# Image 2's norm, the gate's copies and residual's taps, and the order of the attention's sums in a fused mamba, attention and expert kernel

## The chip, the cores and the metric

The kernel runs on one core of a Trainium2 chip. The metric is the device time of one execution in microseconds (us), taken as the median of the runs shown. Each core has TensorE (PE, with weight loads listed apart as PEld), VectorE (DVE), ScalarE (ACT), GpSimd (POOL) and SyncE (SP, which issues most of the transfers here). [...]

## The reference

The input is four images of 256 channels by 1024 positions in float32. Cut to what matters here (LN is a norm over channels):

```python
xs = LN(x)                                     # over the 256 channels, then again with norm_w, norm_b
xc = split(xs into 4 groups of 64 channels)
xm = mamba(xc) + skip * xc                     # selective scan over the 1024 positions
Q  = conv1x1(depthwise3_grouped(xm))           # qdw, qpw
xg = sigmoid(Q) * xm                           # gates
R  = conv1x1(depthwise3(xg)) + xg              # rdw, rpw ("residual")
cat = [xs, R]
xm2 = conv1x1(depthwise3(cat)) + xs            # fdw, fpw ("mixing")
x_out = gelu(LN([depthwise3(xm2), mha(xm2)] @ fc + fc_b))
x  = x + proj(LN(dwconv3x3(LN_hw(x_out))))
t  = tokens(x); x = t + top2_experts(LN(t))    # 8 experts, 256 -> 1024 -> 256
```

`mha` has 8 heads of 32 channels. The mamba scan has, for each group, 128 inner channels by 16 states: `h = exp(dt * A) * h + dt * u * B`, and the output is the sum of `h * C` over the states.

## The kernel before, in words

Channels lie on the 128 partitions in two chunks c (0 and 1), positions along the free axis in two halves h of 512.

**The scan.** For each image b (0 to 3), group n (0 to 3) and half h there is a part of 16 steps i: 32 parts in one long row. A step is four operations on four engines: the decay dA on ACT (L718, an exp of dts), the inflow dBu on DVE (L728, written into a PSUM slot), the scan hs on DVE (L739), and the product of hs with C on POOL (L747). PE adds the products up (L757), spreads B over the partitions (L710), and projects u for the next part (L616, L622). SP loads dts and the C rows ahead (L681, L704). At a part's end ACT copies y out (L764) and POOL multiplies it by z (L765). Each part also prepares the next one: the Silu of u and z (L642, L646, with a table load before and after), and dt (L661 to L668).

**What runs beside it.** Other stages are written as generators. A part's loop advances every running generator after its instructions, and `yield k` means "I have nothing for k ticks". The order of each engine's queue is thus fixed by where the `yield`s stand. `in_turn(items, make, use, lag, every)` issues `make` for an item and `use` for the item `lag` ticks back. The stages of image b run beside image b+1: `convolutions(b)` starts with the first part of image b+1 and mostly falls into the parts (b+1, 0, 0) and (b+1, 0, 1); `attention(b)` starts after a few parts, when the preparation of q, k and v is done. The scan stops while the attention runs and resumes when `attended` is set, three steps before the attention's end. Image 3 has no scan beside it (`beside` is false). Behind it come the expert tiles, from 1676 us to the end.

**Slots.** PSUM tiles come from one ring of 8 banks for everything (`ps`), halves in SBUF from rings of 16 (`a2`) and full rows from 4 (`a4`). A tile that takes a slot waits for the last reader of the tile that had it before.

**Norm.** `normalised(b)`: means by matmul with `ones_mean` (`column_mean`, L438), subtraction on DVE (L536), squares on POOL (L546), variances by L438 again, the root on ACT, then for each chunk a POOL product xl (L556), a DVE product xn (L558), a POOL scale (L561), and for images 2 and 3 `own_taps` (L572 on ACT and twice L579 on DVE; image 3's are taken later from a stored copy). A float32 matmul shows as two records in the trace. The norm of image 1 runs beside the scan, that of image 2 beside attention 0, that of image 3 beside attention 1.

**Gate, residual and mixing.** `convolutions(b)` makes qd on PE (L921), copies it on ACT (qs, L928), multiplies by qpw on PE (gp, L935), copies it on ACT (g, L944), takes the sigmoid (L949), and multiplies xm by the gates on POOL (L957). `depthwise3` then forms residual's three taps: one on ACT (L457) and two on DVE (L462) for each chunk. The projections follow (`rp`, `fx`, `fp`, L426 and L428), with copies on ACT: own L976, residual L994, mixed L968. `prepared` computes v and then q and k, copied on ACT by L1101.

**Attention.** A step is a pair of a group and a half with one of eight key tiles kt: four logit matmuls (L1126), four exps on ACT (L1136), four value matmuls (L1175). DVE adds the exps of an even and an odd step (L1183), and `sum_pair` (L1147) sums the pair on PE with a matmul of ones.

Of the kernel before, what the change touches and what calls it, by code (L numbers as in the profile page):

```python
# [10 lines left out]
AF = mybir.ActivationFunctionType  # L11
ALU = mybir.AluOpType
# [4 lines left out]
NC2 = C // P  # L17
HH = WW = 32
N = HH * WW
# [59 lines left out]
def network(  # L79
# [27 lines left out]
    nc = tc.nc  # L107
    shifted = sums is None
    B = x.shape[0]
# [16 lines left out]
    def col(name, i=0, rows=slice(0, P)):  # L126
        at = _AT[name] + i
        return V[rows, at : at + 1]
# [22 lines left out]
    with tc.tile_pool(name="w_conv", bufs=1) as wp, tc.tile_pool(  # L151
# [248 lines left out]
        def a4(name, shape=(P, N)):  # L400
            return act4.tile(list(shape), F32, tag="a4", name=name)

        def a2(name, rows=P):
            return act2.tile([rows, HALF], F32, tag="a2", name=name)

        def half(h):
            return ts(h, HALF)
# [26 lines left out]
        def column_mean(name, chunks):  # L434

            out = ps(name)
            for ci, chunk in enumerate(chunks):
                nc.tensor.matmul(  # L438
                    out, ones_mean, chunk, start=(ci == 0), stop=(ci == len(chunks) - 1)
                )  # L440
            return out

        def in_turn(items, make, use, lag=2, every=1):

            made, lag = [], lag // every
            for at in range(len(items) + lag):
                if at >= lag:
                    use(items[at - lag], made[at - lag])
                if at < len(items):
                    made.append(make(items[at]))  # L450
                yield every
# [71 lines left out]
        def normalised(b):  # L523


            place_xn(b)
            xn = XN[b]

            def part(c, h):
                return xn[:, c, ds(LEFT + h * HALF, HALF)]  # L530

            yield 4

            def centre(h, mean):
                for c in range(NC2):
                    nc.vector.tensor_tensor(part(c, h), part(c, h), mean, ALU.subtract)  # L536

            yield from in_turn(
                range(2), lambda h: column_mean(f"mean_{b}_{h}", [part(c, h) for c in range(NC2)]),
                centre,  # L540
            )
            r1, r2 = a4(f"r1_{b}"), a4(f"r2_{b}")
            for h in range(2):
                sq = [a2(f"sq_{b}_{h}_{c}") for c in range(NC2)]
                for c in range(NC2):
                    nc.gpsimd.tensor_tensor(sq[c], part(c, h), part(c, h), ALU.mult)  # L546
                yield 1
                var = column_mean(f"var_{b}_{h}", sq)
                yield 2
                root(r1[:, half(h)], var, eps6)  # L550
                yield 1
                root(r2[:, half(h)], var, eps11, scale=1.0 + 1e-5)
                yield 1
            for c in range(NC2):
                xl = a4(f"xl_{b}_{c}")
                nc.gpsimd.tensor_tensor(xl, xn[:, c, LEFT:], r1, ALU.mult)  # L556
                yield 2
                nc.vector.tensor_tensor(xn[:, c, LEFT:], xn[:, c, LEFT:], r2, ALU.mult)  # L558
                yield 1
                nc.sync.dma_start(XL[b][:, c, :], xl)  # L560
                nc.gpsimd.tensor_scalar(  # L561
                    xn[:, c, LEFT:], xn[:, c, LEFT:], col("norm_w", c), col("norm_b", c),
                    ALU.mult, ALU.add,
                )
                yield 1
                if b in XD and b < B - 1:
                    yield from own_taps(b, c, xl)
# [330 lines left out]
        def convolutions(b):  # L898
# [19 lines left out]
            for k in range(3):  # L918
# [5 lines left out]
                        start=(k == 0), stop=(k == 2),  # L924
                    )
                yield 1 if k else 0
            yield 1
            nc.scalar.activation(qs, qd, AF.Identity, bias=qdw_b)  # L928
            yield 1
            def gate(c):  # L930
# [23 lines left out]
            def gating():  # L954
                yield from in_turn(range(NC2), gate, keep)
                for c in range(NC2):
                    nc.gpsimd.tensor_tensor(  # L957
                        xm[:, c, 1 : N + 1], gs[c], xm[:, c, 1 : N + 1], ALU.mult
                    )
                    yield 1  # L960
                for c in range(NC2):
                    yield from depthwise3(d[1], c, xm, c, "rdw_w", c, col("rdw_b", c))

            def mixed(at, r):
                co, h = at
# [48 lines left out]
            for c in range(NC2):  # L1014
                for ticks in depthwise3(
# [11 lines left out]
                    ],  # L1027
                    xl[:, at[0], ds(1 + at[1] * HALF, HALF)] if beside else None,
                    NC2 if beside else 0,
                ), mixed, lag=2 if b == B - 1 else 4, every=1 if b == B - 1 else 2,  # L1030
            )
            yield from prepared(b)

# [73 lines left out]
        def attention(b):  # L1107

            v8, qk = QKV.pop(b)
            rows = [
                largest(b, g, qk[g][:, 0, :], qk[g][:, 1, :]) if shifted else None
                for g in range(2)
            ]
            yield 1
            steps = [(g, h, kt) for g in range(2) for h in range(2) for kt in range(NK)]

            def logits(g, h, kt):  # L1120

                q, k = qk[g][:, 0, :], qk[g][:, 1, :]
                sts = [ps(f"st_{b}_{g}_{h}_{kt}_{i}") for i in range(4)]
                for i in range(4):
                    r = ts(i, HD)
                    nc.tensor.matmul(  # L1126
                        sts[i], k[r, ts(kt, P)], q[r, half(h)], start=True, stop=not shifted
                    )
                    if shifted:
                        nc.tensor.matmul(  # L1130
                            sts[i], ones[HD * i : HD * i + 1, :],
                            rows[g][HD * i : HD * i + 1, half(h)], start=False, stop=True,
                        )
                es = [a2(f"e_{b}_{g}_{h}_{kt}_{i}") for i in range(4)]
                for i in range(4):
                    ins = nc.scalar.activation(es[i], sts[i], AF.Exp, scale=1.0 / HD**0.5)  # L1136
                T["exps"] = ins if b == B - 1 else None
                return es

            log_exp()  # L1140
            ahead = logits(*steps[0])
            pairs, accs, ending = [], [None, None], []

            def sum_pair():
                kt, acc, es = pairs.pop()
                for i in range(4):
                    nc.tensor.matmul(  # L1147
                        acc[ts(i, HD)], ones[:, 0:HD], es[i], start=(kt == 1), stop=(kt == NK - 1)
                    )

            def end_block(g, h, values, total):

                low, out = a2(f"low_{b}_{g}_{h}"), OT[b][g][:, half(h)]
                at = (2 * b + g) * 2 + h
                nc.scalar.activation(low, total, AF.Ln, bias=added)
                if shifted:
                    nc.scalar.activation(low, low, AF.Exp, scale=-1.0)
                else:
                    nc.vector.tensor_reduce(sums[:, 0, at : at + 1], total, AX.X, ALU.max)
                    nc.scalar.activation(  # L1160
                        low, low, AF.Exp, scale=-1.0, accum_out=sums[:, 1, at : at + 1]
                    )
                nc.vector.tensor_tensor(out, values, low, ALU.mult)

            for at, (g, h, kt) in enumerate(steps):
                es = ahead
                if pairs and (kt % 2 or at > len(steps) - 6):
                    sum_pair()
                if at + 1 < len(steps):
                    ahead = logits(*steps[at + 1])  # L1170
                if kt == 0:

                    accs = [ps(f"av_{b}_{g}_{h}_{w}") for w in range(2)]
                for i in range(4):
                    nc.tensor.matmul(  # L1175
                        accs[0][ts(i, HD)], v8[:, kt, ts(4 * g + i, HD)], es[i],
                        start=(kt == 0), stop=(kt == NK - 1),
                    )
                if kt % 2 == 0:
                    first = es  # L1180
                else:
                    for i in range(4):
                        nc.vector.tensor_tensor(first[i], first[i], es[i], ALU.add)  # L1183
                    pairs.append((kt, accs[1], first))
                    if ending:
                        end_block(*ending.pop())
                if kt == NK - 1:
                    ending.append((g, h, *accs))
                if at == len(steps) - 3:
                    T["attended", b] = True  # L1190
                yield 1
            sum_pair()
            yield 1
            end_block(*ending.pop())
            yield 1
# [1324 lines left out]
```

## Time and profile before

| what | value |
|---|---|
| median of 3 runs | 2168.41 us (2166.26 to 2169.15) |
| profiled execution | 2167.03 us, span 2165.3 us |
| granted TensorE clock | 0.961 of full speed |
| attention 0, 1, 2, 3 (from the windows of the trace, about) | 99, 101, 94, 83 us |
| tail of the experts (1676 to 2165 us) | PE busy 458.64 of 489 us |
| L747 POOL product | 512 times, 1339 ns mean |
| L718 ACT decay | 512 times, 718 ns mean |

The page lists each engine's busy time over the whole span, then the span in 40 slices, the costliest groups of instructions, and what ended the idle time before them. A window of the trace gives the same busy times for a stretch. A timeline line gives the start, the duration, the engine, the line of the kernel and its operation, and in brackets the idle time of the engine just before, with what ended it.

### The profile page before, as it was taken

What the parts mean: (1) busy time and instruction counts of PE and PEld (TensorE: products, weight loads), DVE (VectorE), ACT (ScalarE), POOL (GpSimd) and SP (SyncE); (2) the same over time, 40 slices, a digit from 0 to 9 for tenths busy, and PEclk for the clock granted to TensorE, in tenths of its full rate; (3) what the DMA queues carried; (4) which work ended last, traced back from release to release, by engine and by line L of the source; (5) the groups of instructions that cost most, each with busy time, mean ns of one, the idle gap of its engine ahead of it and who ended that gap; (6) DMA issues with size and microseconds to landing.
All of it is one profiled execution on the core that took longest, in us unless ns stands there. A gap on an engine that the chain in (4) does not pass through costs nothing. (4 is left out here: it accounts for less than half of the span.)

```text
span 2165.3 us, 28187 instructions
## 1 busy us (share of the span) xinstructions
PE 1931.0 (89%) x8690; PEld 867.6 (40%) x8690; DVE 1540.5 (71%) x2252; ACT 1212.3 (56%) x2272; POOL 1043.4 (48%) x931
## 2 busy tenths in 40 slices
PE   6778778999977999988779999669999989999996
PEld 2113112322211332223123223216652668888885
DVE  4989999957998989698899888987265354321121
ACT  4665657668777677776466876615268423222221
POOL 0887887812787850476877016662021012522131
PEclk8888999999999999998999999989999999999998
DMA  3555544401444431153634203444230165777764
GB/s 105 148 157 130 124 118 103 101 28 57 103 116 117 104 75 40 25 141 92 176 87 105 83 6 94 109 164 135 84 99 23 47 198 161 242 229 188 213 184 131
DMA packets 157087, 251.40 MB, mean 116 GB/s; under 512 B 34740, under 2 KB 101332, under 8 KB 156664
## 3 DMA queue, kind: packets, MB, share of 16 engines
q1 hardware_dynamic: 136560, 223.47, 37.3%
q0 software_dynamic: 12720, 17.32, 4.1%
q10 hardware_dynamic: 7640, 8.65, 1.2%
q8 instruction: 72, 1.18, 0.2%
q14 instruction: 95, 0.78, 0.1%
HBM read 137.22 MB, written 36.62 MB: 80 GB/s over the span
## 5 line engine op out<-in xcount | busy, mean ns | idle before, releaser
L747 POOL TENSOR_TENSOR dA<-hs,cs 128x512 f32<-128x512 f32 x512 | 681.1, 1339 | 376.9 <-DVE hs L739 249.8
L718 ACT ACTIVATE dA<-dts,A 128x512 f32<-128x512 f32 x512 | 359.0, 718 | 161.4 <-DMA dts<-dt 76.9
L757 PE MATMUL yp<-dA,quads 128*32 128x512 f32 x1024 | 286.3, 640 | 89.3 <-POOL dA L747 76.6
L2350 POOL DMA_INDIRECT Y<-ys,dest x68 | 109.6, 1612 | 424.3 <-DVE ys L2343 417.3
L1136 ACT ACTIVATE e<-st 128x512 f32<-128x512 f32 x512 | 263.7, 606 | 89.4 <-PE st L1126 89.2
L2337 ACT ACTIVATE hs<-h,b 128x256 f32<-128x256 f32 (+1 forms) x256 | 110.6, 478 | 343.6 <-PE h L2332 256.7
L728 DVE TENSOR_TENSOR dBu<-dts,bs 128x512 f32<-128x512 f32 x384 | 259.6, 677 | 46.0 <-PE bs L710 10.8
L739 DVE TENSOR_TENSOR_SCAN hs<-dA,last,dBu 128x512 f32<-128x512 f32 x192 | 243.6, 1269 | 3.0 <-issue 2.1
L2365 PE MATMUL y<-w,hs 128*128 128x256 f32 (+1 forms) x1088 | 242.4, 382 | 0.0
L2332 PE MATMUL h<-xT,w 128*128 128x256 f32 (+1 forms) x1024 | 239.7, 390 | 0.8 <-DVE xT L2295 0.8
L739 DVE TENSOR_TENSOR_SCAN hs<-dA,dBu 128x512 f32<-128x512 f32 x192 | 231.6, 1206 | 0.7 <-PE var L438 0.7
L1183 DVE TENSOR_TENSOR e<-e,e 128x512 f32<-128x512 f32 x256 | 168.2, 718 | 77.8 <-ACT e L1136 47.8
L2332 PEld LDWEIGHTS h<-xT,w 128*128 128x128 f32 x1024 | 195.2, 192 | 41.7 <-issue 8.0
L2365 PEld LDWEIGHTS y<-w,hs 128*128 128x128 f32 (+1 forms) x1088 | 197.3, 188 | 36.1 <-issue 9.0
L2295 DVE COPY xT<-xp 128x512 f32<-128x512 f32 (+1 forms) x36 | 23.3, 646 | 249.4 <-PE xp L2291 249.1
L710 PE MATMUL bs<-u,xpwT_s 128*32 128x512 f32 x1024 | 162.9, 669 | 40.3 <-DVE hs L739 17.3
L1126 PE MATMUL st<-qk 32*128 32x512 f32 x1024 | 174.0, 638 | 0.3
L757 PEld LDWEIGHTS yp<-dA,quads 128*32 128x32 f32 x1024 | 51.3, 114 | 303.4 <-POOL dA L747 198.7
L1175 PE MATMUL av<-e,v 128*32 128x512 f32 x1024 | 139.5, 604 | 0.0
L1953 POOL DMA_INDIRECT XS<-XR,to x64 | 65.4, 1022 | 92.0 <-ACT e L1136 53.9
L1126 PEld LDWEIGHTS st<-qk 32*128 32x128 f32 x1024 | 59.5, 183 | 115.3 <-issue 85.6
L1147 PE MATMUL av<-e,every 128*32 128x512 f32 x512 | 85.2, 596 | 2.7 <-DVE e L1183 2.6
(357 smaller groups left out, 2640.5 us busy)
## 6 DMA issues: line engine op xcount, KB each, us to landing
dts<-dt SPq DMA_DIRECT2D x512, 128.0 KB
w<-in_W_dram SPq DMA_DIRECT2D x124, 512.0 KB
cs<-cd SPq DMA_DIRECT2D x512, 64.0 KB
xs<-XS SPq DMA_DIRECT2D x32, 260.0 KB
xd<-xn SPq DMA_DIRECT2D x64, 128.0 KB
xn<-in_x_dram SPq DMA_DIRECT2D x8, 512.0 KB
XL<-xl SPq DMA_DIRECT2D x8, 512.0 KB
xl<-XL SPq DMA_DIRECT2D x4, 1024.0 KB
```

The costliest lines, as they stand in the source:

```text
L710: nc.tensor.matmul(bs[r], xpwT_s[:, n, s : s + 1].to_broadcast([P, 32]), T[b, n, "u"][:, half(h)], start=True, stop=True,)
L718: nc.scalar.activation(dA, T[b, n, h, "dts", g][:, 0, :], AF.Exp, scale=A[:, g, n, q : q + 1])
L728: nc.vector.tensor_tensor(dBu, T[b, n, h, "dts", g][:, 1, :], T[b, n, h, "bs", q], ALU.mult)
L739: nc.vector.tensor_tensor_scan(hs, T[b, n, h, "dA", i], dBu, 0.0 if h == 0 else last, ALU.mult, ALU.add)
L747: nc.gpsimd.tensor_tensor(dA, hs, T[b, n, h, "cs", q], ALU.mult)
L757: nc.tensor.matmul(T[b, n, h, "yp"][ts(g, 32)], quads, T[b, n, h, "dA", q * GD + g], start=False, stop=(q == GS - 1),)
L1126: nc.tensor.matmul(sts[i], k[r, ts(kt, P)], q[r, half(h)], start=True, stop=not shifted)
L1136: ins = nc.scalar.activation(es[i], sts[i], AF.Exp, scale=1.0 / HD**0.5)
L1175: nc.tensor.matmul(accs[0][ts(i, HD)], v8[:, kt, ts(4 * g + i, HD)], es[i], start=(kt == 0), stop=(kt == NK - 1),)
L1183: nc.vector.tensor_tensor(first[i], first[i], es[i], ALU.add)
L2332: nc.tensor.matmul(hp[:, i, :], w1(c, k0 + i), xT[:, c, :], start=(c == 0), stop=(c == NC2 - 1))
L2365: nc.tensor.matmul(yp[ts(k % parts, n), ts(t % 2, C)], hidden(k)[:, ds(t * P, n)], w2(k), start=(k < parts), stop=(k >= NHC - parts),)
```

## The change

There are four edits.

1. In the norm of image 2 alone, POOL adds the two chunks of each half before the mean and adds the two squares before the variance, so that `column_mean` has one chunk to multiply. The sums use the tiles r1 and r2 in place of four half tiles. The generator takes four more ticks.
2. The qs copy comes one tick later for images 0 to 2. Residual's taps are written out: first tap of chunk 0 on ACT, an idle tick, first tap of chunk 1 on ACT, then four taps on DVE, a tick each.
3. The mixing copies have a lag of 2 in place of 4 for images 0 to 2 (still every second tick).
4. The sum of a pair is issued after the value matmuls of the next step; only for image 2 (`late`) is it issued at the head of the step after that, as it was for all images before.

```diff
@@ normalised(b)
+            r1, r2 = a4(f"r1_{b}"), a4(f"r2_{b}")
+            one_chunk = b == 2
+            if one_chunk:
+                for h in range(2):
+                    nc.gpsimd.tensor_tensor(r1[:, half(h)], part(0, h), part(1, h), ALU.add)
+                yield 2
             yield from in_turn(
-                range(2), lambda h: column_mean(f"mean_{b}_{h}", [part(c, h) for c in range(NC2)]),
+                range(2), lambda h: column_mean(
+                    f"mean_{b}_{h}",
+                    [r1[:, half(h)]] if one_chunk else [part(c, h) for c in range(NC2)],
+                ),
                 centre,
             )
-            r1, r2 = a4(f"r1_{b}"), a4(f"r2_{b}")
             for h in range(2):
-                sq = [a2(f"sq_{b}_{h}_{c}") for c in range(NC2)]
+                if one_chunk:
+                    sq = [v[:, half(h)] for v in (r1, r2)]
+                else:
+                    sq = [a2(f"sq_{b}_{h}_{c}") for c in range(NC2)]
                 for c in range(NC2):
                     nc.gpsimd.tensor_tensor(sq[c], part(c, h), part(c, h), ALU.mult)
+                if one_chunk:
+                    nc.gpsimd.tensor_tensor(sq[0], sq[0], sq.pop(), ALU.add)
+                    yield 1
                 yield 1
                 var = column_mean(f"var_{b}_{h}", sq)
@@ convolutions(b)
-            yield 1
+            yield 2 if beside else 1
             nc.scalar.activation(qs, qd, AF.Identity, bias=qdw_b)
...
+                def first_tap(c):
+                    nc.scalar.activation(
+                        d[1][:, c, :], xm[:, c, 0:N], AF.Identity, bias=col("rdw_b", c),
+                        scale=col("rdw_w", 3 * c),
+                    )
+
+                first_tap(0)
+                yield 1
+                yield 1
+                first_tap(1)
                 for c in range(NC2):
-                    yield from depthwise3(d[1], c, xm, c, "rdw_w", c, col("rdw_b", c))
+                    for k in (1, 2):
+                        nc.vector.scalar_tensor_tensor(
+                            d[1][:, c, :], xm[:, c, k : k + N], col("rdw_w", 3 * c + k),
+                            d[1][:, c, :], ALU.mult, ALU.add,
+                        )
+                        yield 1
...
-                ), mixed, lag=2 if b == B - 1 else 4, every=1 if b == B - 1 else 2,
+                ), mixed, lag=2, every=1 if b == B - 1 else 2,
@@ attention(b)
+            late = b == B - 2
...
-                if pairs and (kt % 2 or at > len(steps) - 6):
+                if late and pairs and (kt % 2 or at > len(steps) - 6):
                     sum_pair()
                 if at + 1 < len(steps):
                     ahead = logits(*steps[at + 1])
...
+                if pairs and not late:
+                    sum_pair()
                 if kt % 2 == 0:
                     first = es
```

## The prediction

> **What bounds the kernel now.** I read the page's busy shares, then a table by stage, then the idle gaps of whichever engine is full in each stage. The chain that ended last is no help: it holds only the final stores. The shares are averages over unlike stages:
>
> ```profile
> PE 1931.0 (89%) x8690; PEld 867.6 (40%) x8690; DVE 1540.5 (71%) x2252; ACT 1212.3 (56%) x2272; POOL 1043.4 (48%) x931
> ```
>
> The table by stage (columns: window, length, busy us and count of PE, PEld, DVE, ACT, POOL, then clock and DMA) for the convolution part of image 0, the scan behind it, attention 0, and the convolution part of image 2:
>
> ```profile
> 332.00:374.00 42.00, 38.71 (x136) 12.30 (x136) 37.08 (x39) 28.49 (x44) 33.90 (x22) 0.96 0.35 85
> 374.00:435.00 61.00, 57.52 (x226) 22.50 (x226) 58.32 (x65) 43.32 (x81) 49.77 (x41) 1.00 0.44 108
> 435.00:534.00 99.00, 98.60 (x650) 27.77 (x650) 64.02 (x84) 75.89 (x147) 15.27 (x11) 1.00 0.09 32
> 1084.00:1128.00 44.00, 37.86 (x131) 11.87 (x134) 39.95 (x38) 27.69 (x43) 34.34 (x29) 0.96 0.34 83
> ```
>
> Read it so: in an attention PE is full (98.60 of 99.00) and POOL nearly idle; in the scan DVE is full (58.32 of 61.00). The convolution parts are the scan with holes in DVE. The holes (timeline of DVE; the bracket is the idle time before and who ended it), for images 0 and 2; image 1 at 690.90 and 704.13 repeats image 0 within 0.1 us:
>
> ```profile
> 332.09 0.69 DVE L728 TENSOR_TENSOR dBu<-dts,bs 128x512 f32<-128x512 f32 x1 [0.22 <-ACT g L944]
> 346.19 1.88 DVE L462 SCALAR_TENSOR_TENSOR d<-xm,V,d 128x1024 f32<-128x1024 f32 x1 [4.02 <-ACT d L457]
> 1083.70 0.70 DVE L728 TENSOR_TENSOR dBu<-dts,bs 128x512 f32<-128x512 f32 x1 [5.42 <-ACT g L944]
> 1096.83 5.43 DVE L462 SCALAR_TENSOR_TENSOR d<-xm,V,d 128x1024 f32<-128x1024 f32 x1 [4.02 <-ACT d L457]
> 1103.97 2.79 DVE L462 SCALAR_TENSOR_TENSOR d<-xm,V,d 128x1024 f32<-128x1024 f32 x1
> ```
>
> So residual's first tap stops the scan for 4.0 us in each of three images, and in image 2 an inflow stops for 5.4 us more. ACT shows why the inflow waits: its own queue stands.
>
> ```profile
> 1075.35 0.69 ACT L928 ACTIVATE qs<-qd,qdw_b 128x512 f32<-128x512 f32 x1 [4.99 <-PE qd L921]
> 331.38 1.25 ACT L944 ACTIVATE g<-gp,V 128x512 f32<-128x512 f32 x2
> 333.49 0.72 ACT L718 ACTIVATE dA<-dts,A 128x512 f32<-128x512 f32 x1 [0.86 <-DMA dts<-dt]
> ```
>
> In attention 0 the var matmuls sit in a full PE, and one block of sums is torn apart (its eight matmuls start at 523.62 and the next logits at 526.65: 3.03 us, where the undisturbed block at 520.69 is followed after 0.97):
>
> ```profile
> 466.35 1.98 PE L438 MATMUL var<-sq,ones_mean 128*128 128x512 f32 x4
> 523.62 1.66 PE L1147 MATMUL av<-e,every 128*32 128x512 f32 x6
> 525.68 1.05 PE L1147 MATMUL av<-e,every 128*32 128x512 f32 x2 [0.40 <-DVE e L1183]
> 526.65 1.14 PE L1126 MATMUL st<-qk 32*128 32x512 f32 x8
> ```
>
> [...] Here the 592 ns var matmuls follow each other every 0.48 us (466.35 to 468.26 for four), so I price them at the pitch. [...] this trace has 1.28. The change adds no load.
>
> **The change, part by part** (in us, minus is faster).
>
> *Norm of image 2, in attention 0.* A mean and a variance per half take one matmul instead of two: four matmuls go, each two records, so eight records of the sixteen. Eight records at 0.48 are 3.8, on a full PE: −3.8. POOL gets four adds of 128x512; its L747 product of that size takes 1.27, so 5.1 in a stage where it is busy 15.27 of 99: hidden. The added ticks push the tail later. In the changed order the second chunk's L558 product and both its L579 taps come after the first steps of the next scan part, where before only the last tap did: two more DVE operations (about 1.2 and 1.28) in a stage where DVE is the bound: +2.4. In return DVE is free at the end of the attention, and the torn block at 523.62 should close: −2.0 (bounds −2.3 and 0). SP's store of XL_2 now stands in its queue among the cs and dts loads of that part and waits for POOL; if a load is held, dA waits: 0 to +3, taken as 0, because loads are issued some steps ahead.
>
> *Sums.* Outside image 2 the sum of a pair is issued at the end of the even step, not at the head of the odd one. Inside an attention that is the same PE order; what changes is that other streams' matmuls (op, mean, var) come behind the sum instead of before it, and that the last inner pairs of the last block are summed one logits-and-values later. At 466.35 var covered 1.98 us in which DVE was adding e (L1183); without that cover the sum can stand at the head of PE: between 0 and 2 per such place, four places in attention 0, most with the adds done long before: +1.5. The late pairs only gain time, counted in the −2.0 above. Attention 1's and 3's stalled sums wait for DVE, which the edit leaves as it is: 0.
>
> *qs copy and g copies.* The qs copy L928 goes behind the table load and Silu, and the first decays. In image 2 it then no longer holds ACT for 4.99. But all gate work comes a step later: on ACT the order becomes dA_2, dA_3, g, g, dA_4, where it was dA_2, g, g, dA_3. The inflow of step 1 takes the PSUM slot of the first gp in both kernels, so it waits for the first g copy. At image 0, dA_3 cannot start before 333.49 (its DMA); 333.49 + 0.72 + one g copy of 0.68 gives 334.9 instead of 332.09: +2.8, and the same for image 1. At image 2 Silu is bound by its up matmuls (L622 ends at 1074.26) once the qs copy no longer stands ahead of it: 1074.3 + 1.15 + 1.08 + 1.29 (Silu, its second line, the load, by the starts 1077.35 to 1080.87) = 1077.8, then dA_0, qs, dA_1, dA_2 and dA_3 at 0.71 each, then one g copy: 1082.0, where the inflow started at 1083.70: −1.7.
>
> *Taps.* In the new order the four DVE taps follow hs6, hs7, hs8, hs9 (before hs4, hs5, hs7, hs8), so the 4.0 in front of the first goes. It doesn't go whole: later xm multiplies put dA's product of step 3 behind z, which waits for ACT's y copy, so hs6 and hs7 wait for slots that POOL frees, and step 5's inflow waits for ACT's L662. I price these at +1.7. For image 0, DVE's path to hs10 (361.50 before): −4.0 (tap) −1.1 (the stretches 1.88 and 1.73 against 1.25) +2.8 +1.7 = −0.6, taken as 0, with −3 and +3 as bounds. Image 1 the same. Image 2: −1.7 −4.0 +1.7 = −4.0, and some of the stretches' 5.7 (5.43 + 2.79 − 2 × 1.25) goes as the taps are spaced: taken as −5 in all, bounds −10 and −1. Image 3 has no scan beside it; PE is nearly full there: 0, bounds ±1.
>
> *Mixing.* With lag 4 the L968 copies and the preparation behind them come a step later; the last L1101 copies run after the last decay, 1.03 apart with PE's matmul between. One of them moves back into the scan. I take half of that pitch, −0.5, in each of three images: −1.5 (bounds −3 and 0).
>
> **Sum.** Norm and sums −3.8 + 2.4 − 2.0 + 1.5 = −1.9; gates and taps −5; mixing −1.5: −8.4. From the profiled execution (span 2165.3, run 2167.03) that gives 2158.6; the median of the runs shown, 2168.41, is 1.4 above it, so on that footing 2160.0.
>
> **Rivals.**
> - *The stalls go whole.* The g copies' +2.8 needs a DMA that lands when it did; if loads come sooner, the three taps give 4.0 + 3.9 + 4.0, image 2's inflow 1.7, the stretches 1.1 twice, mixing 1.5, norm and sums 1.9: −19.2, so 2149.2; with half of image 2's stretches 2146.4. For: the waits named are ACT's and POOL's, which the ticks space out. Against: step 1's slot hangs on the same g copy.
> - *Slower: the g copy takes the place of the tap.* Place: the inflow of step 1 in the part (b+1, 0, 1). Price: +2.8 in three images, with the tap's 4.0 handed to hs6 and hs7 whole, since the gates only end later: +8.4. It decides once new waits exceed the 5.1 per image that taps and stretches free. With norm and sums at −1.9 and mixing at −1.5 the net is +5.0: 2173.4. [...] Against: spaced taps leave scan work to do in the meantime.
> - *No change.* [...] mixing only shifts a wait on PE: −8.4 + 5 + 1.5 = −1.9, so 2166.5.
>
> **How the numbers follow.** Forecast 52%, stalls go whole 17%, slower 18%, no change 13%. What a measurement of this kernel can tell from no change is about 0.2%, 4.3 us: below 2164.1 or above 2172.7. The forecast's own range is 2153 to 2166, with 5 of its 52 points within the bound; the slower rival has 3 of 18 there. Faster 47 + 17 = 64%, same 5 + 13 + 3 = 21%, slower 15%. The range reaches 2148 (between the two times of the stalls gone) and 2173 (the slower case's middle); about 7 in 100 is left out below and 9 above.
>
> **What would show it.** In the changed profile: eight fewer L438 records between 440 and 530, and that attention 3 to 5 us shorter; L558 and both taps of the second chunk inside the part after it, which grows by about 2.4; no idle of 4.0 before residual's first DVE tap (L987 there); the inflow of step 1 waiting about 2.8 for g at image 0 and 1, and less than 5 at image 2; the convolution parts, from the start of their first scan L739 to the end of the last: image 2's shorter than 43.8 (1084.31 to 1128.06) by about 3, as its inflow is counted before it, image 0's and 1's unchanged within 3 from 40.1 and 39.2. I am wrong if image 0's part moves by more than 3 either way, if the attention doesn't shorten, or if the store of XL_2 delays loads.

## The result, and the profile after

The changed kernel took 2175.99 us (median of 9 runs, 2173.28 to 2179.83) against 2168.41 us before (9 runs). The ratio is 1.0039, 95% interval 1.0027 to 1.0052: it is slower by about 8 us, outside the predicted range and on the other side. The profiled executions show the same difference, spans of 2174.2 and 2165.3 us: +8.9.

The busy shares of the page's first part tell almost nothing (TensorE 11 us more busy, yet with eight records fewer):

```profile
PE 1942.2 (89%) x8682; PEld 867.4 (40%) x8682; DVE 1553.0 (71%) x2252; ACT 1211.1 (56%) x2272; POOL 1052.7 (48%) x935
```

So I cut both traces at the same places: the first scan L739 of a part, and the first logit matmul of an attention. Subtracting the start times gives this (us, of the one profiled execution of each kernel; the line numbers of the changed kernel are higher, L739 is L753 there; the images' differences are added up):

| stage | before | after | difference |
|---|---|---|---|
| parts (b+1, 0, *), the gates and taps, images 0, 1, 2 | 77.2, 76.5, 81.3 | 77.0, 77.2, 78.1 | −2.7 |
| from part (b+1, 1, 0) to the first logits, images 0, 1, 2 | 60.4, 60.4, 62.0 | 66.0, 66.1, 65.9 | **+15.2** |
| attention 0 until the scan resumes | 98.7 | 93.0 | −5.7 |
| part (1, 2, 0) behind it | 35.1 | 38.0 | +2.9 |
| part (2, 2, 0) behind attention 1 | 46.1 | 48.8 | +2.8 |
| parts (2, 2, 1) to (2, 3, 1) | 112.6 | 109.8 | −2.8 |
| the rest | | | −0.8 |

The whole loss sits in the second row, the three stages in which mixing and the preparation of v, q and k run beside the scan. I call it the mixing stage. The extra time lies in its first part: part (b+1, 1, 0) takes 36.3 us for image 0, where it took 30.7, and from the first scan of part (b+1, 1, 1) to the first logits both kernels take 29.7.

**The waits at the gates and taps went as worked out.** The idle gaps of DVE in the changed kernel, image 0 (timeline; the bracket is the idle time before):

```profile
333.90 0.70 DVE L742 TENSOR_TENSOR dBu<-dts,bs 128x512 f32<-128x512 f32 x1 [2.67 <-ACT g L958]
342.22 0.69 DVE L742 TENSOR_TENSOR dBu<-dts,bs 128x512 f32<-128x512 f32 x1 [1.00 <-ACT over L676]
347.17 1.28 DVE L753 TENSOR_TENSOR_SCAN hs<-dA,last,dBu 128x512 f32<-128x512 f32 x1 [0.57 <-POOL dA L761]
351.70 1.28 DVE L753 TENSOR_TENSOR_SCAN hs<-dA,last,bs 128x512 f32<-128x512 f32 x1 [0.56 <-POOL dt L682]
```

The 4.02 in front of the first tap is gone, and in its place stand 2.67 behind the g copy (predicted 2.8) and 2.1 in three smaller waits (predicted 1.7). The taps themselves did not go as worked out: residual's four DVE taps of image 0 take 2.17, 2.31, 1.72 and 1.73 us, where they took 1.88, 1.73, 1.25 and 1.25.

**The norm did its part.** The rows of L438 in attention 0 have four var records where eight were; the mean likewise:

```profile
L438 PE MATMUL mean<-r,ones_mean x4: 592/644/697, 460.5 to 465.1; 128*128 128x512 f32 x4
L438 PE MATMUL var<-r,ones_mean x4: 592/644/697, 479.0 to 497.2; 128*128 128x512 f32 x4
```

**The mixing stage.** First the stage's opening in the table by windows, before and then after (the third column from the right is the granted TensorE clock):

```profile
374.00:389.00 15.00, 11.53 (x36) 3.40 (x37) 15.00 (x18) 12.08 (x26) 13.14 (x10) 1.00 0.29 76
```

```profile
374.00:389.00 15.00, 12.85 (x36) 3.12 (x36) 15.00 (x17) 11.62 (x25) 13.07 (x9) 0.66 0.33 83
```

As many matmul records, 36, keep TensorE busy for longer, at a clock of 0.66 on average. TensorE's timeline of the changed kernel shows where:

```profile
376.06 1.12 PE L643 MATMUL zp<-xn,inzT_s 64*128 64x512 f32 x2
378.58 1.85 PE L643 MATMUL zp<-xn,inzT_s 64*128 64x512 f32 x2 [1.39 <-DVE hs L753]
380.38 2.05 PE L426 MATMUL fp<-xl,ident 128*128 128x512 f32 x2
382.22 1.91 PE L428 MATMUL fp<-d4r,fpwT_s 128*128 128x512 f32 x2
384.90 2.08 PE L428 MATMUL fp<-d4r,fpwT_s 128*128 128x512 f32 x2 [0.76 <-DVE d4r L462]
```

The same two zp records take 1.12 us in front of a pause of 1.39 us and 1.85 behind it. Then ACT, where the mixing copies L997 now follow their own products by one step and stand at the head of the queue (before, one of them waited for fp, for 0.9 us), and DVE behind it:

```profile
393.84 0.69 ACT L997 ACTIVATE xl<-fp,V 128x512 f32<-128x512 f32 x1 [3.63 <-PE fp L428]
398.13 0.69 ACT L997 ACTIVATE xl<-fp,V 128x512 f32<-128x512 f32 x1 [2.21 <-PE fp L428]
404.47 0.69 ACT L997 ACTIVATE xl<-fp,V 128x512 f32<-128x512 f32 x1 [4.26 <-PE fp L428]
```

```profile
394.56 0.70 DVE L742 TENSOR_TENSOR dBu<-dts,bs 128x512 f32<-128x512 f32 x1 [1.15 <-ACT xl L997]
399.22 0.69 DVE L742 TENSOR_TENSOR dBu<-dts,bs 128x512 f32<-128x512 f32 x1 [1.14 <-PE bs L724]
```

Three suspects come out of these lines: the mixing lag (the waits on ACT), the qs tick (everything behind it is a step later), and the clock.

### The profile page after: what moved, and what is told of

The parts are those of the page before. It is cut to its first block, busy times and chain, and to the rows that moved or that the text cites. A ratio compares the mean times of both kernels' runs of the same rounds, so it can differ in the third digit from the quotient of the medians.

```text
span 2174.2 us, 28190 instructions
## 1 busy us (share of the span) xinstructions
PE 1942.2 (89%) x8682; PEld 867.4 (40%) x8682; DVE 1553.0 (71%) x2252; ACT 1211.1 (56%) x2272; POOL 1052.7 (48%) x935
## 5 line engine op out<-in xcount | busy, mean ns | idle before, releaser
L771 PE MATMUL yp<-dA,quads 128*32 128x512 f32 x1024 | 291.2, 636 | 81.4 <-POOL dA L761 72.6
L742 DVE TENSOR_TENSOR dBu<-dts,bs 128x512 f32<-128x512 f32 x384 | 259.7, 677 | 63.3 <-PE bs L724 12.9
L753 DVE TENSOR_TENSOR_SCAN hs<-dA,last,dBu 128x512 f32<-128x512 f32 x192 | 243.5, 1268 | 7.0 <-ACT dA L732 3.5
L753 DVE TENSOR_TENSOR_SCAN hs<-dA,dBu 128x512 f32<-128x512 f32 x192 | 231.7, 1207 | 1.3 <-PE av L1177 1.3
L742 DVE TENSOR_TENSOR bs<-dts,bs 128x512 f32<-128x512 f32 x128 | 86.1, 672 | 0.9 <-DMA dts<-dt 0.9
```

The lines of the kernel that those rows point to most:

```text
L742: nc.vector.tensor_tensor(dBu, T[b, n, h, "dts", g][:, 1, :], T[b, n, h, "bs", q], ALU.mult)
L753: nc.vector.tensor_tensor_scan(hs, T[b, n, h, "dA", i], dBu, 0.0 if h == 0 else last, ALU.mult, ALU.add)
L771: nc.tensor.matmul(T[b, n, h, "yp"][ts(g, 32)], quads, T[b, n, h, "dA", q * GD + g], start=False, stop=(q == GS - 1),)
```

## The experiments

Each ratio is to runs of the kernel before made beside the kernel on the same chip, with its 95% interval; it can differ a little from the quotient of the two medians. Stage times come from one profiled execution of each kernel. "Lost clock" is my sum over windows of 2 us in the mixing stage, of 2 us times what the granted clock was below 1.

### The edits alone, and the change without its mixing lag

**mix_only**: the kernel before with

```diff
-                ), mixed, lag=2 if b == B - 1 else 4, every=1 if b == B - 1 else 2,
+                ), mixed, lag=2, every=1 if b == B - 1 else 2,
```

> The kernel before with the mixing copies' lag of 2 alone. Theory A (the copies, one step behind their own matmuls, stand at the head of ACT and hold the decays): each of the three parts (b+1, 1, 0) grows by some 5 us, 12 to 15 us slower in all, with ACT waiting 2 to 4 us for PE fp in front of each copy, and TensorE's granted clock stays at 1.0 there. Theory B (the half TensorE clock between 378 and 389 comes from the gate and tap edit, and makes the products late): within 2 us of before, no long waits for fp.

2173.26 us, ratio 1.0018 (1.0007 to 1.0029). The mixing stages took 63.7, 63.6 and 62.0 us, with the waits for fp that theory A foresaw (5.67 and 4.26 us), but the clock fell too. By the ratio that is 3.9 us: a third of what theory A wanted, and more than theory B allows. The attentions took 99.7, 97.8 and 90.0 us, 0.9 longer each.

**no_mix**: the changed kernel with that line as it was.

> The changed kernel with the mixing lag back at 4. Theory A: the 15 us of the three parts (b+1, 1, 0) and (b+1, 1, 1) go, so about 2161, 7 us faster than before. Theory B: the clock is still at half for some 10 us in these parts and most of the loss stays: 2168 to 2176.

2175.71 us, ratio 1.0039 (1.0026 to 1.0052): the changed kernel's time. The stages took 65.8, 65.2 and 65.0 us, with 5.1, 5.1 and 1.7 us of lost clock (this execution took 2180.63, 5 us over the median). The opening for image 0:

```profile
374.00:389.00 15.00, 12.17 (x35) 3.29 (x37) 15.00 (x17) 10.99 (x22) 12.79 (x8) 0.73 0.36 94
```

So the lag alone is not the cause: with it taken back, nothing comes back.

**norm_only**: the first edit alone, all of its hunks in `normalised`.

> The kernel before with the norm of image 2 on one chunk alone. If the term was right: attention 0 shorter by 4 to 6 us, part (1, 2, 0) longer by 2 to 3, together 1 to 4 us faster than before. Rival: the gain of attention 0 belongs to the order of the sums, and this kernel is 2 to 3 us slower.

2167.80 us, ratio 0.9993 (0.9982 to 1.0004). In its trace attention 0 is 4.4 us shorter and part (1, 2, 0) 2.0 longer, as expected. The whole gain, 1.5 us, is too small to be told from none.

**gate_only**: the second edit alone (qs tick and written-out taps).

> The kernel before with the qs tick and the spaced taps alone. Theory A: the convolution parts as in the changed kernel (0 to 2 us shorter for images 0 and 1, about 3 us ahead at image 2's), nothing lost behind them: 3 to 6 us faster. Theory B: TensorE's clock falls to half behind them and the parts (b+1, 1, 0) grow by several us: 5 us slower or more.

2173.00 us, ratio 1.0026 (1.0017 to 1.0035). The convolution parts are 0.8 us shorter for image 0 and 3.2 for image 2, and the mixing stages behind them longer: 63.3, 64.9, 64.9 us, with 1.7 us of lost clock each. Theory A of this run is refuted, and theory B's 5 us or more came (5.6). This edit, without the mixing lag, carries most of the loss.

### Which half of the gate edit

**qs_only**: the kernel before with

```diff
-            yield 1
+            yield 2 if beside else 1
             nc.scalar.activation(qs, qd, AF.Identity, bias=qdw_b)
```

> The kernel before with the qs tick alone. Theory C (the tick makes everything behind it one scan step later, so that two more copies of q and k run after the last decay and the attention starts some 2 us later in each image): this kernel holds most of the gate edit's loss, 5 to 9 us slower than before, with the stall of 4 us at residual's first tap still there and a gap of some 2 us between the last scan and the first logits. Rival D (the loss comes from the spaced taps): within 2 us of before.

2171.87 us, ratio 1.0017 (1.0007 to 1.0027). The mixing stages took 64.9 us in all three images. TensorE's timeline at the end of the stage, before and then qs_only:

```profile
433.93 1.06 PE L757 MATMUL yp<-dA,quads 128*32 128x512 f32 x8
434.93 2.93 PE L1126 MATMUL st<-qk 32*128 32x512 f32 x16
```

```profile
435.70 1.07 PE L757 MATMUL yp<-dA,quads 128*32 128x512 f32 x8
436.70 1.99 PE L428 MATMUL qkp<-xl,wqkT_s 128*128 128x512 f32 x4
438.61 2.93 PE L1126 MATMUL st<-qk 32*128 32x512 f32 x16
```

Before, the logits (st) follow the last sums of the scan (yp) at once. With the tick one more q and k product (qkp) stands between, 1.9 us after the scan has nothing left to do. The tick at qs, some 110 us earlier, has pushed the end of the whole chain past the end of the scan. By the ratio the loss is 3.7 us, less than the 5 to 9 expected; theory C's sign holds, and rival D's 2 us lies just inside the interval. One expectation failed: the stall of 4 us at residual's first tap is gone here too (0.94, 0.93 and 0.93 us), with the taps as they were.

In the changed kernel the place is another one. There the logits follow the scan's sums at once, as before, because the smaller lag has taken the last product back into the scan (image 0):

```profile
439.44 1.06 PE L771 MATMUL yp<-dA,quads 128*32 128x512 f32 x8
440.43 2.94 PE L1155 MATMUL st<-qk 32*128 32x512 f32 x16
```

So the product behind the scan is what the tick costs with the old lag; with the new one the time is lost earlier, in part (b+1, 1, 0).

**taps_only**: the kernel before with residual's taps written out as in the change.

> The kernel before with the spaced taps alone, the qs copy where it was. Theory C: the 4 us at the first tap shrink in three images, the inflow does not wait for the g copies, and the attention starts no later after the last scan: 3 to 10 us faster. Rival D: 4 to 6 us slower, as the gate edit as a whole.

2166.63 us, ratio 0.9994 (0.9983 to 1.0006). That is 1.3 us of gain, not told from none: less than theory C wanted, and far from rival D. The wait in front of the first tap is short even without the qs tick, and in image 0 no inflow waits for the gates (in image 2 one still waits 5.43 us, as before). DVE, image 0:

```profile
347.23 1.28 DVE L739 TENSOR_TENSOR_SCAN hs<-dA,last,dBu 128x512 f32<-128x512 f32 x1 [1.14 <-ACT dA L718]
349.39 1.88 DVE L973 SCALAR_TENSOR_TENSOR d<-xm,V,d 128x1024 f32<-128x1024 f32 x1 [0.87 <-ACT d L962]
```

The convolution parts are 1.5 and 1.2 us shorter for images 0 and 1 and 1.6 longer for image 2. In this execution the mixing stages took 60.4, 63.7 and 63.7 us, the last two with 3.4 us of lost clock each; nothing in the edit tells image 0 from image 1.

**sums_only**: the fourth edit alone.

> The kernel before with the order of the sums alone. Theory C: the part (2, 2, 0) behind attention 1 starts its inflows later because spread_b stands behind the sums on TensorE: 46.1 us become about 48.8 from its first scan to that of the next part; attention 0 gains 1 to 2 us; in all 1 to 3 us slower. Rival: within 1 us of before, so that the change's loss is all of the gate edit and the mixing.

2169.23 us, ratio 1.0002 (0.9992 to 1.0012): nothing in all, as the rival has it. Inside there are movements that cancel. Attention 0 with the part behind it is 1.7 us shorter and attention 3 is 1.3 shorter. Part (2, 2, 0) is 2.8 longer. ACT at the end of attention 1, and DVE behind it, sums_only and then before:

```profile
898.78 1.57 ACT L1136 ACTIVATE e<-st 128x512 f32<-128x512 f32 x3 [4.74 <-PE av L1148]
```

```profile
900.38 0.70 DVE L728 TENSOR_TENSOR dBu<-dts,bs 128x512 f32<-128x512 f32 x1 [6.69 <-ACT e L1136]
894.09 0.70 DVE L728 TENSOR_TENSOR dBu<-dts,bs 128x512 f32<-128x512 f32 x1 [3.09 <-ACT e L1136]
```

The exps of the last steps wait 4.74 us for a sum that now stands one logits-and-values later, and the inflow waits 6.69 us for them where it waited 3.09. That spread_b stands behind the sums, as I expected, isn't what the lines show.

**norm_taps**: the norm edit and the taps together.

> The norm of image 2 and the spaced taps together, without the qs tick, the mixing and the sums. Theory C: the gains add, 4 to 12 us faster than before. Rival D: 2 to 5 us slower.

2163.57 us, ratio 0.9978 (0.9968 to 0.9987): faster than both kernels by the 4 to 12 us that theory C wanted (4.8), though its profiled execution lost clock in all three mixing stages (63.7, 62.0, 63.7 us).

### The clock

Over all these executions the lost clock of a mixing stage took only four values: 0, 1.7, 3.4 and 5.1 us. Among the kernels without the qs tick, every stage of 60.4 us lost none, but for one whose dip began 2.5 us after its first scan; every one of 62.0 lost 1.7, and every one of 63.6 or 63.7 lost 3.4. That includes the first stage of sums_only, whose edit lies in the attentions behind it.

The clock records of these traces show when it fell. In them the clock is at half (0.50) or full (1.00): 31 stretches at half in the kernel before, 33 in the changed one. Each lasts 3.41 us or a whole multiple of it, up to 6 × 3.41, but for the last one, which reaches past the program's end; and within one execution all of them start on one grid of 3.41 us. In the changed kernel, for example, the stretches of 10.24 us that start at 378.85 and 740.67 lie 106 × 3.41 us apart. The falls in the windows of the nine other executions that show any fit in the same way. From execution to execution the grid lies differently to the program. Image 2 before, cut along its grid:

```profile
1135.03:1138.44 3.41, 1.62 (x4) 0.59 (x4) 3.41 (x5) 1.53 (x4) 2.71 (x2) 1.00 0.00 0
1138.44:1141.85 3.41, 3.41 (x11) 0.70 (x10) 3.41 (x6) 1.74 (x5) 3.41 (x4) 0.50 0.09 22
1141.85:1145.27 3.42, 3.42 (x14) 1.02 (x13) 3.42 (x6) 2.57 (x6) 3.42 (x4) 1.00 0.25 55
```

One stretch of 3.41 us at half clock is the step of 1.7 us. TensorE was busy for 1.62 of the 3.41 us in front of this fall. The longest pause just ahead of the fall was 1.39 us in the changed kernel (above) and 2.10 us in norm_taps.

In the kernels without the tick this pause of 2.10 us comes 5.0 to 7.1 us after the stage's first scan, and the kernel before has it at images 0 and 1 too, with no fall. The grid tells these cases apart in all 21 stages of the seven kernels with neither tick nor added work. Where a step of the grid began 4.0 to 5.1 us after the first scan, the stage lost 3.4 us of clock behind the pause (nine stages); 5.3 to 5.6, 1.7 us (five); 5.9 to 6.8, nothing (seven, one of them with the earlier dip in place of the pause). So the same instructions have three times here (60.4, 62.0 and 63.7 us), and which one goes with where the grid happens to stand.

To test whether the pauses do it, TensorE was given something to do in them: the same product is written into the same bank again, which changes no result.

```diff
-            nc.tensor.matmul(
-                zp, inzT_s[rows, c, :], XN[b][rows, c, ds(LEFT + h * HALF, HALF)],
-                start=True, stop=True,
-            )
+            for _ in range(3 if b and n == 2 and h == 0 else 1):
+                nc.tensor.matmul(
+                    zp, inzT_s[rows, c, :], XN[b][rows, c, ds(LEFT + h * HALF, HALF)],
+                    start=True, stop=True,
+                )
```

**after_fill**: the changed kernel with this, and in `product` for fp_0_0

```diff
             if kept is not None:
+                again = name.startswith("fp_") and name.endswith("_0_0")
+                for _ in range(2 if again else 0):
+                    nc.tensor.matmul(out, ident, kept, start=True, stop=True)
                 nc.tensor.matmul(out, ident, kept, start=True, stop=False)
```

> The changed kernel, and in each part (b+1, 1, 0) the first zp matmul and the first matmul of fp_0_0 made three times instead of once (the same product into the same bank, results unchanged), which puts some 4 us of work into TensorE's two pauses there. Theory E (a pause of 1.4 to 2.1 us there lets the granted clock fall to half, and the three parts lose as many us as the clock loses): the clock stays at 1.00 between 4 and 16 us after the part's start, the stage from this part to the attention falls from 66 to 61 to 63 us in each image, and the kernel is 6 to 14 us faster than the changed one: 2162 to 2170. Rival F (the half clock only goes along; the waits for the products of fp set the time): the same 2174 to 2178, or slower by the added matmuls.

2173.34 us, ratio 1.0016 (1.0006 to 1.0026), where the change has 1.0039. The stages took 64.1 us in all three images, no clock lost. Some 5 us are back (0.0023 of 2168), less than the 6 to 14 of theory E, whose 61 to 63 us for the stage were not reached either. Rival F, for which the clock only goes along, is refuted by the stages; but it names waits for fp beside the clock, and 64.1 is still 3.7 above 60.4. These 3.7 us lie in part (b+1, 1, 0): 34.4 us against 30.7. ACT still waits for fp there (1.67, 2.21 and 4.26 us for image 0), and one DVE tap of d4r, 1.81 us, has come over from the part before.

**before_fill** and **norm_taps_fill**: the kernel before, and norm_taps, with the zp repetition alone.

> The kernel before with the first zp matmul of each part (b+1, 1, 0) made three times (results unchanged). Theory E: the same 60.4 us in all three stages whatever the moment of the run; 1 to 4 us faster than before in the median, as before loses 0, 0 and 1.7 us in the profiled run and more in others. Rival F: within 1 us, or slower by up to 6.

> The norm of image 2 and the spaced taps alone, with the first zp matmul of each part (b+1, 1, 0) made three times (the same product, results unchanged). Theory E: no loss of clock in the three parts, each stage at 60 to 61 us (63.7, 62.0 and 63.7 without it), 2157 to 2161, and a smaller spread of the runs. Rival F: 2163 to 2166.

before_fill: 2166.17 us, ratio 0.9975 (0.9966 to 0.9985). norm_taps_fill: 2161.05 us, ratio 0.9958 (0.9942 to 0.9975), the fastest version here. All six stages took 60.4 us. norm_taps_fill lies at the upper edge of theory E; it has only 6 runs, and its profiled execution is the fastest of them. By the ratio before_fill is 5.4 us faster than before, more than the 1 to 4 expected. The opening of the stage by windows, before_fill: 44 records where before has 36, four of them the added ones (the part starts 0.8 us later here, so that others fall into the window), and a full clock.

```profile
374.00:389.00 15.00, 12.89 (x44) 3.84 (x39) 15.00 (x17) 11.89 (x24) 13.14 (x9) 1.00 0.31 83
```

Without added work, 6 of 33 mixing stages lost no clock; with it, in the five kernels that have it, all fifteen.

How much of the change's loss is clock? With the added work in both, the changed kernel is still slower by 0.0041, 8.9 us (1.0016 against 0.9975; 2175.39 and 2166.57 us in the profiled executions). That is the whole loss. The added work gains 5.0 us in the changed kernel and 5.4 us in the kernel before, each within 2 to 4 us. So by these runs the clock costs both kernels about the same, and no part of the 8 us is shown to be its doing; the execution of the kernel before that was profiled happened to lose little.

**after_no_qs**: the changed kernel without the qs tick.

> The changed kernel without the qs tick. Theory C (the tick costs some 3 us in each stage from part (b+1, 1, 0) to the attention, in the combination too): these stages fall from 66 to 62 to 64 us, the inflow no longer waits for the g copies, and the kernel is 5 to 9 us faster than the changed one: 2167 to 2171. Rival: the tick only makes up for the mixing copies, and nothing or less than 2 us is gained.

2171.49 us, ratio 1.0003 (0.9989 to 1.0018): the loss against before is gone, which by the ratios is 8 us of gain on the changed kernel, as theory C has it. The stages took 63.7, 63.7 and 60.4 us, with 3.4, 3.4 and 0 us of lost clock: on the line of the kernels without the tick. No inflow waits for the g copies at images 0 and 1; at image 2 one still waits 5.16 us. The third stage compares with after_fill, both at a full clock: 60.4 against 64.1 us.

### The tick and the lag with the clock held

**qs_fill** (qs_only with both repetitions) and **mix_fill** (mix_only with that of zp).

> The kernel before with the qs tick and with the same added TensorE work as in after_fill (zp and the first matmul of fp_0_0 three times, results unchanged). Theory G (two separate costs: the tick puts a last q and k product behind the scan, some 3 us per image whatever the clock; the clock's falls come on top): no loss of clock in the three stages, each at 62.5 to 64 us against 60.4 in before_fill, and the kernel 5 to 9 us slower than before_fill. Rival H (the tick costs only through the clock): each stage at 60.4 to 61.

> The kernel before with the mixing lag of 2 and the first zp matmul of each part (b+1, 1, 0) three times (results unchanged). Theory G (the lag alone costs nothing before the attention, its longer stages were the clock's; it costs 0.9 us in each attention): stages at 60.4 to 61, attentions 0, 1 and 2 at 99.7, 97.8 and 90.0 us, 2 to 4 us slower than before_fill. Theory A (the copies' wait for their own products costs of itself): stages at 63 us or more in spite of a full clock.

qs_fill: 2169.51 us, ratio 1.0011 (1.0002 to 1.0021), stages of 63.4, 63.4 and 63.3 us. mix_fill: 2166.37 us, ratio 0.9992 (0.9981 to 1.0003), stages of 60.4 us in all three. The openings by windows, qs_fill and then mix_fill, both at a full clock:

```profile
374.00:389.00 15.00, 14.41 (x50) 4.77 (x48) 15.00 (x16) 10.96 (x22) 12.95 (x8) 1.00 0.34 92
```

```profile
374.00:389.00 15.00, 12.90 (x50) 3.62 (x43) 15.00 (x18) 11.52 (x23) 12.46 (x8) 1.00 0.31 82
```

Theory G holds in the stages. With the clock full, the tick costs 3.0 us per image (63.4 − 60.4), 1.5 of it in part (b+1, 1, 0), and the lag nothing before the attention; attentions 0, 1 and 2 took 99.7, 97.8 and 90.0 us with it, 0.9 more each. qs_fill has the repetition of fp as well, before_fill has not; but qs_only (and gate_only at images 1 and 2), with the tick and neither repetition, took 64.9 us with 1.7 us of lost clock, which leaves 2.8 for the tick if a dip costs no more than it loses. By the ratios qs_fill is 7.8 us slower than before_fill (1.0011 against 0.9975) and mix_fill 3.7 us, both as expected.

## Why the prediction was wrong, and where it was right

In the profiled executions the +15.2 of the mixing stage splits so: 3 × 3.7 = 11.1 stays with the clock full (64.1 in after_fill against 60.4), of which the tick alone makes 3 × 3.0 = 9.0; the clock makes 1.9 + 2.0 + 1.8 = 5.7 (66.0, 66.1, 65.9 against 64.1), less the 1.6 that the profiled execution before lost itself at image 2. By the ratios the clock cancels between the kernels, and the 11.1 are what turned the sign: the prediction had −1.5 there. Without the clock and its −2.8 the rows of the first table come to −2.7 + 11.1 − 5.7 + 2.9 + 2.8 = +8.4.

- **The step that failed** is in "qs copy and g copies". I wrote that all gate work comes a step later and followed the delay only to hs10 of the same part. The work behind it (d4r's taps, then fp, v, q, k) comes a step later as well, and that I put at nothing. With the old lag the chain's end, the L1101 copies, was already running past the last decay, and one product more runs behind the scan (qs_only). With the new lag part (b+1, 1, 0) is 3.7 us longer instead; removing the tick from the changed kernel brings the stage back to 60.4 at a full clock (after_no_qs). How these 3.7 divide between the d4r tap, the waits for fp and the rest no run shows.
- **Mixing** (−1.5): the copies did move back into the scan, but with the clock held the lag gave 0 before the attention (mix_fill), though ACT waits for fp there (2.43 and 4.26 us for image 0). With the tick beside it the stage is 0.7 longer per image than with the tick alone (64.1 against 63.4; after_fill has the other edits too). The 0.9 us that the lag costs in attentions 1 and 2 of mix_fill does not show in the changed kernel (97.0 and 89.1 us; 96.9 and 89.1 before).
- **No term for the clock.** The windows that I quoted show 0.96 and 1.00 in neighbouring stages, and I read them as a property of the chip. It moves a stage by 1.6 or 3.3 us where the instructions are the same, but it isn't what made the change slower.
- **Norm and sums, attention 0 and the part behind it** (predicted −4.3 and +2.4): −5.7 and +2.9. The sum is near, with luck in its terms. The sums, priced at +1.5 in the attention, gain there: sums_only is 2.9 us shorter. The norm, with the torn block at −5.8, gains 4.4 alone; the two gain less together than the sum of each alone. Behind the attention the norm adds 2.0 and the sums 1.2.
- **Sums elsewhere**: attention 1 at 0 was wrong, part (2, 2, 0) behind it gave +2.8; the gains in attention 0 and 3 balance it.
- **g copies** (+2.8 at images 0 and 1): the waits are 2.67 and 2.19. Right.
- **Taps** (images 0 and 1 at 0, image 2 at −5): −0.2, +0.7, −3.2, within the bounds, again with luck. The 4.0 in front of the first tap goes by either half of the gate edit alone. The stretches were to give 1.1 per image; the four taps became longer instead, by 1.8 us for image 0 (7.93 against 6.11) and 1.9 for image 2 (12.64 against 10.72). That POOL's work beside a tap stretches it was my estimate, on which the rival "no change" rested too. No run shows it apart, and in the kernel before POOL was busy for 1.04 and 1.10 us beside taps that took 1.25 (318.44 and 377.35). Image 2's gain comes with the tick (3.0 in qs_only), while the written-out taps alone cost 1.6 there; by the prediction's own sign, the part's first scan to the end of its last, image 2's went from 43.8 to 42.7, not down by 3.
- **The slower rival** named the g copy as the place. The sign came true, the place did not: that wait was the predicted 2.8 and was paid for by the tap's 4.0.

The −2.8 of the parts (2, 2, 1) to (2, 3, 1) goes with the clock too. All of it lies in part (2, 3, 0), which took 42.3 to 42.5 us in the six executions where the half clock ran 3.5 us or more into its start (before and after_fill among them), 40.9 where it ran 0.8 us into it (norm_only), and 39.4 or 39.5 in the nine where its start had the full clock (after and before_fill among them). No run was made that holds the clock there.

## What to carry to other kernels

In a hand-ordered pipeline, follow a delay to the end of its chain, not to the stall that it was made for: here a tick that costs nothing where it stands was paid for in the next stage, at the chain's end or inside the scan, depending on the lag behind it. The mixing stage, whose TensorE pauses lie just ahead of the clock's falls, had three times here (60.4, 62.0 and 63.7 us) where the instructions were the same, so compare single stages with the granted clock beside them before blaming an edit, and hold the clock in both kernels before giving it a share of a difference. Here the repeated matmuls in such a pause gained 5.4 us (before_fill), about as much as the best of the edits (norm_taps, 4.8).

## What was not expected of the hardware

TensorE's clock fell to half behind pauses of 1.39 and 2.10 us, for 3.41 us or a multiple of it, on a grid that lay differently to the program in each execution. In the kernels without the tick it cost the stage as much as it lost: 1.7 us gave 1.6, 3.4 gave 3.3. It did not always: in the changed kernel 5.1 us gave 1.9, and in norm_only a dip in the first six us of a stage gave nothing. Four added records of matmul work per image, some 1.7 us (by after_fill, where eight zp records in a row take 3.70 us and two in the changed kernel 1.12), took it away in the three mixing stages of before_fill, and that kernel was 0.25% faster than the one before (interval 0.15 to 0.34%).
